# First operands of four stages made in the stages in front, zeros set in parts by VectorE, two norms in one, and VectorE's order in a quantised FFN

## The chip, the cores and the metric

The kernel runs on one core of one Trainium2 chip. The core has a matrix engine (TensorE, PE in the profile), a vector engine (VectorE, DVE), an engine for activation functions (ScalarE, ACT), a general engine (GpSimd, POOL), and a queue engine (SyncE, SP) that issues most transfers between device memory and the on-chip memory SBUF. TensorE writes its results to PSUM. The metric is the time of one execution on the device in microseconds (us), as the median of several runs.

## The reference

The input x is 2048 tokens of 256 numbers, and ctx is a context of the same size. Eight sublayers follow each other, each added to x behind a layer norm without weights:

```
x = x + gamma * cross_attention(norm(x), ctx)             # 8 heads               stage A
x = x + (silu(n @ gate * s) * (n @ up * s)) @ down * s    # 704 wide, ternary     stage B
x = x + quantised_cross_attention(norm(x), ctx)           # 16 heads, 8-bit       stage C
x = x + h + a, a = causal_attention(norm(h)), h = norm(x) # 16 heads of 128       stage D
      + moe(norm(h + a))                                  # 4 experts, top 2
x = x + banded_attention(norm(x), ctx)                    # 8 heads, band of 64   stage E
x = x + bit_linear(silu(w1) * w2, w3)(norm(x))            # 1024 wide, quantised  stage F
x = x + V @ sigmoid(Q^T K)(norm(x), ctx)                  #                       stage G
x = x + moe(norm(x)) + shared(norm(x))                    # 8 experts, top 2      stage H
```

The norm divides by sqrt(variance + 1e-5). Stage D takes two norms in a row: norm(x), and over it a norm with weight and bias. In F each linear layer first takes a root-mean-square norm with a gain, scales the row so that its largest entry becomes 127 (the largest is held at 1e-4 or above), rounds, multiplies by a matrix of -1, 0 and 1, and scales back.

## The kernel before, in words

Tokens lie in 16 tiles `xs[i]` of 128 tokens by 256 numbers that stay in SBUF through the whole kernel, and so do 16 tiles `cs[i]` of the context. Feed-forward stages work on four groups of four tiles (`NG`), with tokens as the matmul's free axis, so they need transposed normed tokens `xnT`. The stages run in the order of `STAGES`; F and G are fused in `run_F`, and `run_G` then returns at once.

The main loop (from L1673) opens the pool of the next stage's weights at the start of the present stage, and its loads are queued on SP there. Pools of successive stages lie on alternate sides of SBUF (`side_of`, L68), counted over all eight letters. As G has a letter of its own, F and H lie on one side, and H's weights are loaded when F is over.

Every engine executes its instructions in the order in which the program issues them. Most stages are therefore written as Python generators that issue a few instructions a step, and a loop over slots steps them beside each other. Where the code says `manual_schedule`, the written order stands; buffers named alike in a pool share memory and wait for each other.

- A (`run_A`, L403): the slots come from `attention_slots` (L330). `start(t)` is called once per slot.
- B (`run_B`, L466): per group, `norm_T` (L505) makes statistics, the normed tiles and their transposes; then six chunks `ic` of the hidden layer with products gp and up, and the down products op (L495). Beside it run keys and values of C (`keys_and_values`, L542), one step at the start and one behind each chunk: product kvp (L568), quantised keys, transposes kTp, kT; at the end the values are scaled by their largest entry (vall, L617) and spread over the zeroed tile vz (L621). vz is zeroed at once by GpSimd (L554).
- C (`run_C`, L644): `queries(i)` (L675) makes the quantised queries of tile i in ten steps; the loop over 256 pairs of tile and head has scores (L759), a row maximum and exponentials on VectorE (L789), ScalarE (L813) and GpSimd (L823), a transposing transfer, and products with vz (L772). `output(i)` (L722) ends a tile.
- D (`load_D` L840, `run_D` L854, `run_D_attention` L920): `inputs(g)` (L934) makes the two norms of one group, one after the other, and the transposes hnT; `values` (L964), `projections` (L974). `run_D_moe` (L1072) has the experts: `hidden(n)` (L1084) and `output(n)` (L1096) for group and expert n, `routed_D` for the next group's routing; beside them run two generators: `tern`, which makes F's ternary matrices (`ternary`, L1260, with a transfer fw, a sum of absolute values L1271, tanh and rounding), and `first`, which makes E's first operands (`first_of_E`, L1169). The latter zeroes and fills eight halves of stk and stq by GpSimd (`operand_buffers`, L148, its line L153).
- E (`run_E`, L1209) uses the same attention slots as A.
- F and G (`run_F`, L1301): software pipeline; a list `parts` (L1505) gives the order of the parts in a period and each one's lag in tiles. `deviations` takes the variance, `scales` (L1335) the scale factors, `first_sizes` (L1345) xk and its largest entries, `gained` (L1404) multiplies the hidden row by its gain on GpSimd (xr, L1409), `second_norm` (L1411) and `second_rounding` (L1417) treat the hidden row.
- H (`load_H` L1557, `run_H` L1578): `owner`, a constant of experts by columns, is built by a memset and six selects on GpSimd (L1586 to L1590); `routed(g)` (L1597) makes a group's norm, transposes, gates and shares; then 14 chunks with pgate and pup (L1649), a broadcast cb of the shares (L1653), and `down` (L1626).

The order of the experts of D around `output`:

```
                next(first if n > 6 else tern, None)
                if e in (1, 2, 3):
                    next(routing, None)
                output(n)
                next(routing, None)
                next(tern, None)
                next(first, None)
```

Of the kernel before, what the change touches and what calls it, by code (L numbers as in the profile page):

```python
# [31 lines left out]
def tile_net(ctx: ExitStack, tc: tile.TileContext, a: dict, out: bass.AP):  # L32
# [31 lines left out]

    beside = []
    pending = []

    def side_of(stage):  # L68
        return ("left", "right")[STAGES.index(stage) % 2]


# [76 lines left out]
    def operand_buffers(pool, k, b, eng=None):  # L148

        pair = {}  # L150
        for kind, value in (("k", 1.0), ("q", 0.0)):
            pair[kind] = pool.tile([P, 16, D], BF, name=f"st{kind}{b}")
            (eng or V).memset(pair[kind][64:P], value)  # L153
        k.setdefault("st", []).append(pair)
# [248 lines left out]
    def run_A(w, side):  # L403
        with ExitStack() as es:
# [6 lines left out]
            masks = []  # L411

            def prepare(i):
# [9 lines left out]
                if i < 4:  # L423
                    operand_buffers(cp, k, i)
# [5 lines left out]
            def start(t):  # L430
                if t in (16, 18):
                    next(parts)
                if t == 20:
                    for r in range(2):
                        masks.append(cp.tile([P, 1], F32, name=f"gmask{r}"))
                        V.tensor_tensor(masks[r], k["mask"][r], w["gamma"], ALU.mult)

# [16 lines left out]
    def load_B(wp):  # L454
# [8 lines left out]
        w["down_s"] = bcast_row(wp, a["L0_ffn_down_s"], D, "sdown")  # L463
        return w

    def run_B(w, side):  # L466
        with tc.tile_pool(name="Bw", bufs=2, side=side) as pool, tc.tile_pool(
            name="Bp", bufs=1, space=PSUM
        ) as psum:
            other, stats = beside.pop() if beside else (iter(()), iter(()))  # L470
            next(other, None)
            for g in range(NG):
                ids = range(4 * g, 4 * g + 4)
                xnT = norm_T(pool, psum, ids)
                hT = pool.tile([P, 6, 512], F32, name="hT")
                for ic in range(6):
# [13 lines left out]
                    next(other, None)  # L490
                for j, i in enumerate(ids):
# [8 lines left out]
                    G.tensor_tensor(xs[i], xs[i], t, ALU.add)  # L500
                next(stats, None)
            for _ in other:
                pass

    def norm_T(pool, psum, ids, src=None, wb=None, keep=None):  # L505
# [3 lines left out]
        xnT = pool.tile([P, 2, 512], F32, name="xnT")  # L509
        for j, i in enumerate(ids):  # L510
# [5 lines left out]
            dst = xnT[:, :, j * P : (j + 1) * P]  # L516
            if wb is None:
                S.copy(dst, tp)
            else:
                for c in range(2):  # L520
                    S.activation(
                        dst[:, c, :], tp[:, c, :], AF.Identity, bias=wb[1][:, c : c + 1], scale=wb[0][:, c : c + 1]
# [4 lines left out]
    def load_C(wp):  # L527
        w = {}
        w["q"] = load(wp, [P, 2, D], a["L1_xattn_Wq"].rearrange("(c p) n -> p c n", p=P), "wq")
        w["kv"] = load(wp, [P, 2, 2 * D], a["L1_xattn_Wkv"].rearrange("(c p) n -> p c n", p=P), "wkv")  # L530
# [7 lines left out]
        w["bkv"] = bcast_row(wp, a["L1_xattn_bkv"], 2 * D, "bkv")  # L538
        w["bp"] = load(wp, [1, D], a["L1_xattn_bp"], "bp")
        w["norm"], w["stats"] = {}, query_stats(w)  # L540
        beside.append((keys_and_values(w), w["stats"]))
        return w  # L542

    def keys_and_values(w):
# [9 lines left out]
        G.memset(vz, 0.0)  # L554
        w["spread"] = spread = qkp.tile([H, 4, 2, 64], F32, name="spread")
        with tc.tile_pool(name="C1v", bufs=1, side=side) as vp, tc.tile_pool(
            name="C1w", bufs=2, side=side
        ) as pool, tc.tile_pool(name="C1p", bufs=1, space=PSUM) as psum:
            vall = vp.tile([P, NT, D], F32, name="vall")
            vm = vp.tile([P, D], F32, name="vmax")  # L560
            V.memset(vm, 0.0)
            for i in range(NT):
# [30 lines left out]
                V.tensor_copy(kT[:, :, i * P : (i + 1) * P], tb)  # L593
                yield
# [1177 lines left out]
```

## Time and profile before

| | us |
|---|---|
| median of 3 runs (2830.92 to 2835.79) | 2834.84 |
| the profiled execution | 2838.68 |
| its span | 2837.0 |
| TensorE busy | 2441.6 (86%) |
| VectorE busy | 1892.7 (67%) |
| ScalarE busy | 1531.6 (54%) |
| GpSimd busy | 1560.0 (55%) |
| A / B / C begin at | 0 / 299 / 531 |
| D's attention / experts begin at | 1229 / 1846 |
| E / F with G / H begin at | 2016 / 2332 / 2522 |

A timeline row has the start in us from the span's start, the duration in us, the engine, the line, the operation, output and input tiles, their shapes, how many like instructions are drawn together (x4), and in brackets how long the engine was idle just before and which instruction ended that. The page also has a table of 40 slices of the span: each digit is the busy share of an engine in tenths, and in the row PEclk the granted clock of TensorE in tenths.

### The profile page before, as it was taken

The page shows a single profiled execution, that of the slowest core. Times are in us where ns is not written, and L with a number is a line of the kernel's source. Part 1 is how long each engine was busy: PE and PEld are TensorE (multiplying, and loading weights), DVE is VectorE, ACT ScalarE, POOL GpSimd, SP SyncE. Part 2 cuts the span into 40 slices and gives each one's busy share as a digit, 9 for nine tenths or more (in the row PEclk, how much of TensorE's full clock was granted, in tenths as well). Part 3 has the DMA queues.
Part 4 walks back from the last instruction along what each step waited for, and adds up shares of the span by engine and source line. Part 5 has one row for each costly group of instructions (what it writes and reads, how often), then busy time and mean ns, then how long its engine had stood idle before and what let it go on. Part 6 is the DMA issues. An engine that isn't in the chain of part 4 may idle for free.

```text
span 2837.0 us, 44436 instructions
## 1 busy us (share of the span) xinstructions
PE 2441.6 (86%) x16072; PEld 1437.3 (51%) x16072; DVE 1892.7 (67%) x3961; ACT 1531.6 (54%) x2186; POOL 1560.0 (55%) x1733
## 2 busy tenths in 40 slices
PE   4989798777787787779999999979898876779999
PEld 2545344344444444336666666746555543445555
DVE  7877555699999999955554555654577759933322
ACT  1667221499999999836555555424255456721111
POOL 4655433488888888856555555442488865630000
PEclk9999799899999999979999999989999999989999
DMA  6553000499999999920000000010343400020000
GB/s 167 134 116 71 23 1 1 85 204 200 205 203 202 200 202 205 206 86 8 16 8 23 8 1 1 15 45 25 83 96 88 95 21 1 1 77 8 8 8 8
DMA packets 610599, 223.70 MB, mean 79 GB/s; under 512 B 547366, under 2 KB 600524, under 8 KB 605772
## 3 DMA queue, kind: packets, MB, share of 16 engines
q1 hardware_dynamic: 607308, 220.07, 35.4%
q8 instruction: 127, 2.08, 0.3%
q10 hardware_dynamic: 3072, 0.79, 0.2%
q14 instruction: 92, 0.75, 0.1%
HBM read 66.91 MB, written 18.87 MB: 30 GB/s over the span
## 4 chain that ended last, share of the span: by engine, by line
PE 48%; DVE 22%; issue 9%; POOL 7%; ACT 2%; DMA 1%; ACTq 0%; DVEq 0%; POOLq 0%; SPq 0%
DVE e L789 11%; PE yp L1042 4%; PE ppq L983 4%; PE ppk L983 4%; PE hout L1628 3%; PE vp L971 3%; PE pgate L1649 3%; PE pup L1649 3%; POOL e L286 2%; PE ep L1104 2%; PE sp L1001 2%; PE op L1027 2%; PE hmp L1091 2%; PE sc L759 1%; PE op L495 1%
## 5 line engine op out<-in xcount | busy, mean ns | idle before, releaser
L813 ACT ACTIVATE ei<-e,nb,sq 128x2048 int16<-128x2048 f32 x256 | 535.4, 2092 | 44.4 <-DVE nb L810 40.8
L823 POOL CAST eb<-ei 128x2048 bf16<-128x2048 int16 x256 | 482.4, 1895 | 117.2 <-ACT ei L813 101.8
L759 PE MATMUL sc<-kT,qz 128*128 128x512 bf16 x1024 | 298.3, 382 | 140.4 <-DVE e L789 138.1
L246 DVE TENSOR_REDUCE negm<-s 128x2 f32<-128x512 f32 (+1 forms) x512 | 300.8, 611 | 127.0 <-PE s L242 123.6
L789 DVE TENSOR_SCALAR_CACHE_REDUCE e<-sc,mx 128x1024 f32<-128x1024 f32 x256 | 326.1, 1274 | 0.8 <-DVE nb L810 0.7
L789 DVE TENSOR_SCALAR_CACHE_REDUCE e<-sc 128x1024 f32<-128x1024 f32 x256 | 312.4, 1220 | 11.5 <-PE sc L759 10.5
L278 ACT ACTIVATE e<-s 128x1024 f32<-128x1024 f32 (+1 forms) x256 | 233.2, 915 | 149.9 <-PE s L274 115.5
L242 PE MATMUL s<-stk,stq 96*128 96x256 bf16 (+1 forms) x1024 | 191.5, 270 | 40.9 <-DMA d3k<-t3k 24.4
L759 PEld LDWEIGHTS <-qz 128*128 128x128 bf16 x1024 | 94.8, 97 | 259.7 <-issue 201.1
L991 POOL TENSOR_TENSOR rwq<-rwq,sin 128x512 f32<-128x512 f32 x64 | 81.2, 1268 | 235.6 <-ACT rwq L988 211.7
L274 PE MATMUL s<-stq,stk 128*128 128x256 bf16 (+1 forms) x1024 | 180.0, 261 | 9.4 <-DMA stq<-nm 4.7
L772 PEld LDWEIGHTS <-vz 128*64 128x64 bf16 x4096 | 123.0, 110 | 115.5 <-issue 115.5
L772 PE MATMUL av<-eT,vz 128*64 128x128 bf16 x4096 | 163.7, 222 | 8.5 <-DMA eT<-eb 8.4
L1003 DVE TENSOR_REDUCE mx<-sp 128x4 f32<-128x512 f32 x64 | 44.3, 692 | 189.9 <-PE sp L1001 189.9
L988 ACT ACTIVATE rwq<-ppq,dbq 64x512 f32<-64x512 f32 x128 | 87.4, 683 | 150.4 <-DVE rtq L985 147.0
L1659 DVE TENSOR_TENSOR hm<-pup,sl 128x512 f32<-128x512 f32 (+1 forms) x56 | 38.7, 692 | 190.4 <-PE pup L1649 186.6
L242 PEld LDWEIGHTS <-stq 96*128 96x128 bf16 x1024 | 93.4, 100 | 135.6 <-issue 111.4
L296 PE MATMUL o<-e,vmo 128*32 128x256 f32 (+1 forms) x2048 | 150.7, 367 | 7.4 <-POOL e L286 6.0
L87 POOL TENSOR_TENSOR rstd<-ve,mhalf 128x1 f32<-128x1 f32 (+1 forms) x52 | 38.1, 733 | 209.3 <-DVE ve L85 90.0
L1657 ACT ACTIVATE sl<-pgate 128x512 f32<-128x512 f32 (+1 forms) x56 | 33.4, 597 | 218.7 <-PE pgate L1649 218.7
L286 POOL TENSOR_SCALAR_AFFINE_SELECT e<-e 128x256 f32<-128x256 f32 (+1 forms) x256 | 133.2, 547 | 30.3 <-ACT e L278 30.1
L971 PE MATMUL vp<-Dwv,hnT 128*128 128x512 f32 x256 | 123.7, 605 | 4.0 <-ACT hnT L946 4.0
(369 smaller groups left out, 5521.8 us busy)
## 6 DMA issues: line engine op xcount, KB each, us to landing
stk<-d3k SPq DMA_DIRECT2D x96, 192.0 KB
stq<-d3q SPq DMA_DIRECT2D x96, 192.0 KB
d3k<-t3k SPq DMA_DIRECT2D x160, 64.0 KB
d3q<-t3q SPq DMA_DIRECT2D x96, 64.0 KB
eT<-eb SPq DMA_TRANSPOSE x256
fw<-in_L_ffn_w SPq DMA_DIRECT2D x3, 1024.0 KB
x<-in_x SPq DMA_DIRECT2D x16, 128.0 KB
c<-in_ctx SPq DMA_DIRECT2D x16, 128.0 KB
```

The lines of the kernel that those rows point to most:

```text
L242: PE.matmul(sc[:, hh, lo:hi], qs[0:96, 2 * hp + hh, qc * P : (qc + 1) * P], ks[0:96, 2 * hp + hh, lo:hi], start=band is None, stop=True, s ...
L246: V.tensor_reduce(negm[:, qc, 2 * hp : 2 * hp + 2], sc[:, :, lo:hi], AX.X, ALU.max, negate=True)
L274: PE.matmul(sc[:, c, lo:hi], ks[:, h, lc * P : (lc + 1) * P], qs[:, h, lo:hi], start=True, stop=True)
L278: S.activation(e[:, :, lo:hi], sc[:, :, lo:hi], AF.Exp, scale=scale)
L286: G.affine_select(e[:, :, s0:s1], e[:, :, s0:s1], [[0, 4], [step, s1 - s0]], ALU.is_ge, 0.0, base=base, channel_multiplier=chan,)
L759: PE.matmul(sc[:, k0 : k0 + 512], qz[i % 2][:, h, :], kT[:, h // 2, 1024 * part + k0 : 1024 * part + k0 + 512], start=True, stop=True,)
L772: PE.matmul(av[i][r0 : r0 + 64, h // 4, :], vz[:, kt, h // 4, h % 4, :], eT[:, kt, :], start=h == 0 and kt < 2, stop=h == H - 1 and kt >= ...
L789: V.tensor_scalar(e, scs.pop((n, part)), 1.0, mx[:, 0:1] if part else LOWEST, ALU.mult, ALU.max, accum_out=mx[:, part : part + 1],)
L813: S.activation(ei, es_.pop(n), AF.Exp, bias=nb, scale=sq[i][:, h : h + 1], accum_out=sums[i][:, h : h + 1],)
L823: G.tensor_copy(eb, eis.pop(n - 1))
L971: PE.matmul(vp, hnT[g][:, c, j * P : (j + 1) * P], wv[:, c, :], start=c == 0, stop=c == 1)
L983: PE.matmul(pp, wt[:, c, hh * P : (hh + 1) * P], hnT[g][:, c, :], start=c == 0, stop=c == 1)
```

## The change

1. **First operands ahead.** A dictionary `heads` holds generators that a stage's loader leaves for the stage in front. B's first group (`norm_parts`) is stepped in A's slots from t = 146; C's first tile (`queries_of_C`, with zeroing of qz and scaling of the weights) at the end of the generator that runs in B; D's first group (`inputs_D`) in C's tail from n = 256 and between the steps of the last `output`; H's first group (`routed_H`) in F's tail from t = 17.
2. **Sides.** They are counted over "ABCDEFH", so F and H lie on opposite sides and H's weights are loaded while F runs. `owner` is made by three copies on ScalarE from the identity matrix. In H, the routing of the next group is issued in steps, one a chunk, from chunk 3.
3. **B.** vz is zeroed a tile at a time, in each step of `keys_and_values`. Its last part is split by more yields, and `run_B` calls it more often at its end (two steps a chunk in the last group, one behind each of the last eight outputs, one more at g = 1). wkv and bkv are loaded by the generator.
4. **D's norms.** `inputs_D` takes one set of statistics per tile: with variance v, the second norm's factor follows from (v + 1e-5) * 1e-5 + v. One pow makes both factors. The expert weights we1, be1, be2 are loaded behind the first group's attention weights instead of in front of them; the first columns of wv are loaded with the stage's small weights.
5. **D's experts.** E's zeros and ones are set by VectorE, one memset per step. `output` is split in two halves, and `another()` steps one generator behind the hidden layer and behind each half. `ternary` issues the next matrix's load earlier, and takes its sum in two halves.
6. **F.** The scale factors are made by a pow and a multiplication on GpSimd (`factors`), with the constants folded in; `scales` has two VectorE instructions less with two operands. The order of `parts` is changed.

The diff, cut to its core:

```diff
+    SEQ = STAGES.replace("FG", "F")
     def side_of(stage):
-        return ("left", "right")[STAGES.index(stage) % 2]
+        return ("left", "right")[SEQ.index(stage) % 2]
+    heads = {}
...
-    def operand_buffers(pool, k, b, eng=None):
+    def operand_buffers(pool, k, b):
...
-            (eng or V).memset(pair[kind][64:P], value)
+            V.memset(pair[kind][64:P], value)
+            yield
...
+                if t == 146 and "B" in heads:
+                    head.append(heads.pop("B")(pool, psum))
+                if head:
+                    next(head[0], None)
...
+        w["xnT0"] = wp.tile([P, 2, 512], F32, name="xnT0")
+        heads["B"] = lambda pool, psum: norm_parts(w["xnT0"], pool, psum, "tp", range(4))
...
+                if g == 1:
+                    next(other, None)
-                xnT = norm_T(pool, psum, ids)
+                xnT = norm_T(pool, psum, ids, dst=None if g % 2 else w["xnT0"], bufs=1) if g else w["xnT0"]
...
-                    next(other, None)
+                    for _ in range(2 if g == 3 else 1):
+                        next(other, None)
...
+                    if g >= 2:
+                        next(other, None)
...
+    def norm_parts(dst, pool, psum, tag, ids):
+        mv, rstd = ln_stats(pool, [xs[i] for i in ids], "hd")
+        yield
+        for j, i in enumerate(ids):
+            xn = pool.tile([P, D], F32, name="hdn", bufs=2)
+            ln_apply(xn, xs[i], mv, rstd, j)
+            yield
+            S.copy(dst[:, :, j * P : (j + 1) * P], transpose_to(psum, xn, tag, f"hdT_{i}"))
+        yield
...
-        G.memset(vz, 0.0)
...
                 V.tensor_copy(kT[:, :, i * P : (i + 1) * P], tb)
+                G.memset(vz[:, i], 0.0)
                 yield
...
+        for b in range(2):
+            V.memset(w["qz"][b], 0.0)
+        S.mul(w["q"], w["q"], 0.25)
+        S.mul(w["bq"], w["bq"], 0.25)
...
+            yield from queries_of_C(w, 0, pool, qzp, psum)
...
-                for _ in queries(0):
-                    pass
...
+                    if n == N and "D" in heads:
+                        own = dict(stats=(small, H, "amq"), bn=(small, H, "rsq"), h0=(pool, D, "xn"), h1=(pool, D, "qq"))
...
+                        head = heads.pop("D")(tile, psum)
+                    if n >= N:
+                        next(head, None)
                 for _ in out_:
+                    next(head, None)
+                for _ in head:
                     pass
...
+    def inputs_D(w, hs, hnT, g, tile, psum):
...
+            V.bn_stats(b6, xs[4 * g + j])
+            V.bn_aggr(mv[:, j, :], b6)
...
+        V.tensor_scalar(ve[:, 0, :], mv[:, :, 1], 1e-5, None, ALU.add)
+        V.scalar_tensor_tensor(ve[:, 1, :], ve[:, 0, :], 1e-5, mv[:, :, 1], ALU.mult, ALU.add)
+        G.tensor_tensor(r, t[:, 8:16], mhalf[:, 0:8], ALU.pow)
...
             ahead = routed_D(w, hs, 0, pool, psum, "vy")
             weights_of(0)
-            inputs(0)
+            if "D" in heads:
+                heads.pop("D")
+                inputs(0)
+            else:
+                mv, rstd = ln_stats(pool, [xs[j] for j in range(4)])
+                for j in range(4):
+                    ln_apply(hs[j], xs[j], mv, rstd, j)
+                    G.tensor_tensor(hs[j], hs[j], w["bo"], ALU.add)
+            w["experts"]()
...
+            def another():
+                q = next(slots)
+                next(tern if q % 8 >= 4 and q < 24 or q == 24 else first, None)
...
-                next(first if n > 6 else tern, None)
+                another()
...
-                output(n)
+                output(n, 0)
+                another()
+                output(n, 1)
                 next(routing, None)
-                next(tern, None)
-                next(first, None)
+                another()
...
+            def factors(t, n, nm):
+                r = pool.tile([P, 1], F32, name=f"r{nm}")
+                G.tensor_tensor(r, t[:, n : n + 1], mhalf[:, 0:1], ALU.pow)
+                f = pool.tile([P, n + 1], F32, name=f"f{nm}")
+                G.tensor_scalar(f, t, r, 1.0, ALU.mult, ALU.mult)
+                return f
+            def scales(am, f, n, nm):
-                V.tensor_scalar(am, am, s, 1e-4, ALU.mult, ALU.max)
+                V.tensor_scalar(am, am, 1.0 / 127.0, f[:, n : n + 1], ALU.mult, ALU.max)
                 sc = pool.tile([P, n], F32, name=f"sc{nm}")
                 V.reciprocal(sc, am)
-                V.scalar_tensor_tensor(sc, sc, 127.0, s.to_broadcast([P, n]), ALU.mult, ALU.mult)
                 dq = pool.tile([P, n], F32, name=f"dq{nm}", bufs=4)
-                V.tensor_tensor(dq, am, at_, ALU.mult)
+                V.tensor_tensor(dq, am, f[:, 0:n], ALU.mult)
...
             parts = [
                 (summed, 5), (first_transposes, 1), (first_copy, 1), (second_transposes, 4), (second_copy, 4),
-                (hidden, 2), (g_product, 7), (g_sum, 7), (hidden_products, 1), (gates, 1), (second_norm, 3),
-                (squares, 2), (gained, 2), (g_context, 6), (g_context_copy, 6), (first_sizes, 0), (first_rounding, 0),
-                (second_rounding, 3), (g_scores, 6), (g_tanh, 6), (output, 4), (deviations, -1), (g_norm, 5),
+                (second_factors, 3), (first_sizes, 0), (hidden, 2), (g_product, 7), (g_sum, 7), (hidden_products, 1),
+                (gates, 1), (squares, 2), (gained, 2), (g_context, 6), (g_context_copy, 6), (first_rounding, 0),
+                (second_sizes, 3), (deviations, -1), (g_deviations, 5), (second_rounding, 3), (first_factors, -1),
+                (g_norm, 5), (g_scores, 6), (g_tanh, 6), (output, 4),
             ]
...
+                    if with_g and t >= NT + 1 and part.__name__ == "gained":
+                        next(heads.get("owner", head), None)
+                    if with_g and t >= NT + 1 and "H" in heads:
+                        head = heads.pop("H")(pool, psum, ("l0", "l1"), "sl")
+                    if t >= NT + 1 and part.__name__ in ("g_sum", "g_tanh"):
+                        next(head, None)
...
+    def owners(owner):
+        for t in range(3):
+            rows = slice(32 * t, 32 * t + 32)
+            S.copy(
+                owner[rows].rearrange("p (e i) -> p e i", i=176), bc(ident[rows, 32 * t : 32 * t + 8], 2, [32, 8, 176])
+            )
+            yield
...
-                    if ch == 5 and g + 1 < NG:
-                        nxt = routed(g + 1)
+                    if ch == 3 and g + 1 < NG:
+                        nxt = routed_H(w, g + 1, pool, psum, ("tp", "tp"), "xn4")
+                    next(nxt, None)
```

## The prediction

> **What bounds the kernel now.** I read the page's table of slices first, for where TensorE goes slack, then the timeline around each of those places.
>
> ```profile
> PE   4989798777787787779999999979898876779999
> ...
> PEclk9999799899999999979999999989999999989999
> ```
>
> One slice is 70.9 us. TensorE is nearly full over long stretches; it is lower between stages, in F (slices 32 to 35) and in C (7 to 17), where VectorE sets the pace at 2.56 us a head and nothing is changed. The change works on the seams and on F, so the sum goes seam by seam.
>
> ```profile
> 298.60 13.75 POOL L554 MEMSET vz<- 128x16384 bf16 x1
> 301.04 11.34 DVE L85 TENSOR_SCALAR ve<-mv 128x4 f32<-128x4 f32 x1
> 330.80 2.07 PE L482 MATMUL gp<-xnT,wgate 128*128 128x512 f32 x4
> ...
> 520.88 0.72 POOL L500 TENSOR_TENSOR x<-x,t 128x256 f32<-128x256 f32 x1 [2.84 <-DVE t L499]
> 530.89 1.23 DVE L789 TENSOR_SCALAR_CACHE_REDUCE e<-sc 128x1024 f32<-128x1024 f32 x1 [5.65 <-PE sc L759]
> ...
> 1217.86 0.72 POOL L752 TENSOR_TENSOR x<-x,ops 128x256 f32<-128x256 f32 x1
> 1229.11 1.92 PE L971 MATMUL vp<-Dwv,hnT 128*128 128x512 f32 x2
> ...
> 1862.17 7.28 DVE L91 TENSOR_SCALAR hn<-h,mv,rstd 128x256 f32<-128x256 f32 x2 [0.74 <-POOL rstd L87]
> 1865.64 3.65 POOL L153 MEMSET stq<- 64x4096 bf16 x1
> 1869.88 3.78 PE L1104 MATMUL ep<-we,hm 128*128 128x256 f32 x8 [6.38 <-DVE h L1107]
> ...
> 2401.34 0.42 DVE L1326 BATCH_NORM_STATS2 b<-x 128x6 f32<-128x256 f32 x1
> 2406.79 2.49 POOL L1409 TENSOR_TENSOR xr<-h,fg 128x512 f32<-128x512 f32 x2
> 2407.01 1.06 DVE L1340 SCALAR_TENSOR_TENSOR sca<-sca,s 128x2 f32<-128x2 f32 x1
> 2410.69 0.42 DVE L1326 BATCH_NORM_STATS2 b<-x 128x6 f32<-128x256 f32 x1
> ...
> 2503.12 0.72 POOL L1503 TENSOR_TENSOR x<-x,gy 128x256 f32<-128x256 f32 x1 [3.01 <-ACT gy L1502]
> 2521.92 3.76 PE L1649 MATMUL pgate<-xnT,hwgate 128*128 128x512 f32 x4
> ```
>
> The blocks are the seams A to B, B to C and C to D, D's experts, F's loop, and the seam to H. Each seam shows the last operation of the old stage or the load in the way, then the first of the new. The bracket is idle time of that engine and what ended it. Two things stand out: a tiny VectorE instruction takes 11.34 us beside the 13.75 us GpSimd memset (the same 128x4 operation takes 0.15 at 313.69), and 7.28 us cover two multiplies that take 0.73 elsewhere (1226.53) beside GpSimd memsets of 3.5. So each large GpSimd memset holds VectorE for its length.
>
> **The change, part by part**, against the profiled execution of 2838.68 us (span 2837.0), which is 3.84 us above the median 2834.84.
>
> **A to B, 26 us.** The first group's norm, transposes and zeros leave the head of B. A's last chain ends with VectorE's reciprocal of the denominators at 295.06, so with xnT0 made in A's tail the first gp can start at about 296 instead of 330.80: 34.8 us. TensorE was not empty in that gap: keys and values of context tiles took about 8 us there (three products kvp of 1.9 each, transposes), which now stand in B's loop. That loop was 102.0 of 110 us busy from 350 to 460, so I hide none of it: 34.8 - 8 = 26.8, less about 1 for the norm's small instructions in A's tail. The memset becomes 16 parts of about 13.75/16 = 0.86, each holding VectorE that long at most, under a loop in which VectorE had 61.2 and GpSimd 40.2 of 110 busy; queued behind each piece on GpSimd is the next tile's kk, which came 0.5 to 3 us after idle time there, so I cost the pieces at nothing, and at 16 x 0.86 = 14 if that cover fails. The load of wkv, now issued by the generator itself, is still ahead of its first use on SP's queue (the first kvp waited 4.33 us for it at 299.85, inside the gap); it stays hidden if issued while A runs. Bounds: 15, if the pieces wait in A's tail or VectorE's holds reach TensorE, and 31, if half of the 8 goes into gaps and TensorE stays warm (it had a granted clock of 0.58 from 294.7 to 330.8).
>
> **B to C, 8.3 us.** The last x of B starts at 520.88, the first e at 530.89. Zeros, scaling and queries of tile 0 now run in B's tail, so what is left is the last product, the release of its PSUM and one score chunk (529.82 to 530.89, 1.07): about 522.5. Against it, ten query steps are added to B's tail, where the splitting of the values left TensorE 5.65 us idle in 460 to 482 (16.35 of 22). I count the two as level. Bounds 5 to 9.
>
> **C to D, 6 us.** Last x to first vp: 11.25 us. Both norms in one take out one round of statistics, a pow (1.0) and a multiply; for group 0 the chain leaves D's head. But its steps share with C's last output the one small PSUM buffer, so C's tail becomes longer: I put the first vp at about 1223. Bounds 1 (the chain only moves ahead of the last output) and 11 (all of it hidden). The moved loads: the expert weights no longer stand in SP's queue in front of the attention's; Dwv's first columns are there early, Dwq is then the one that may be late.
>
> **D's experts, 15 us.** E's eight memsets go from GpSimd to VectorE: four of 3.47 and four of 1.77 (rows of the same tiles in A), 20.9 us of VectorE time, one per slot. VectorE then has some 40 us of work in the first expert group against 33.5 for TensorE. Without GpSimd's locks (7.28, 4.59 and others), with output split in two and the ternary weight fetched ahead (a reduce waited 7.70 us for its DMA at 1898.26), I walk the first group to 54 us instead of the 69.5 from its first product to the next group's. Groups behind took 34 to 41 and stay. Bounds 5 (VectorE's memsets cost as much as the locks did) and 25 (down to the later groups' length).
>
> **E's start, 4 us.** Its first statistics at 2021.05 wait 3.81 us and a score 5.27; with E's first operands done earlier, this goes. Bounds 0 to 6.
>
> **F, 12 us.** A period is 9.35 us (2401.34 to 2410.69) and VectorE is 94% busy in it. The row sca shows the loss: 1.06 us beside GpSimd's xr, where scb, blocked by nothing, takes 0.16. In the new order no two-operand VectorE instruction lies under xr, and two scale multiplies move to GpSimd (0.21 to 0.28 each there). VectorE's period in the new order: 9.35, less 0.90 for the blocked sca, less 0.32 for two multiplies of 0.16 that leave it, plus 0.29 for longer forms of those that stay (an estimate), 8.42, so 0.93 a period; the loop over TensorE and ScalarE needs 8.0 to 8.4 and limits any more. 15 periods are 14; I take 12, as the first and last are not bound by VectorE. Bounds 0 and 17.
>
> The Trainium skill has the rule behind this ("SBUF — State Buffer", section "Who interferes with whom"): VectorE's second port pair is GpSimd's, a VectorE instruction with two SBUF inputs is shut out by a GpSimd one that reads SBUF, and "not with one that only writes it". sca agrees. The rule also speaks against the change: the new factors are GpSimd reads and stand in front of xk, which has two SBUF inputs. That result is rival 1.
>
> **F to H, 15 us.** TensorE's last product in F ends at 2502.4 and pgate starts at 2521.92: 19.5. H's weights (5.44 MB, 2503.9 to 2522) now load during F, when DMA stood at 0.00 of its share, and routing for group 0 runs in F's tail; the owner tile's selects on GpSimd (11 us) become three copies on ScalarE. About 1.5 more as the cold first pgate (3.76, later 1.88) is warm. Against it F's tail gets the routing's pieces, a table load of 1.28 (perhaps two) and copies of some 1.4 on the engine that closes the loop (an estimate between 0.60 for 512 elements, L1657, and 2.09 for 2048, L813): 6. Bounds 9 and 22.
>
> **Sum**: 26 + 8.3 + 6 + 15 + 4 + 12 + 15 = 86.3. 2838.7 - 86.3 = 2752 on the profiled scale, 2749 with the 3.84 us to the median; I say 2750.
>
> **Rivals.**
> 1. The ports shut each other out in F in another place: GpSimd's factors beside VectorE's xk. For it: 0.5 us of GpSimd multiplies a period are new there. Against it: at 2358.50 a pair of xk kept its usual 0.87 beside a GpSimd pow of 0.72 (0.55 elsewhere), so little is lost. F then gains nothing: 2762.
> 2. The heads are made early but the next stage still waits, for memory or PSUM of the old pools or for the weights that are loaded behind it. For it: at 1218.61 the statistics waited for the very last x though group 0 was long done. Half of the four seams' 55 us is lost, and some of D's: 2750 + 28 + 10 = 2788. This is also the case that the change does not do what it says.
> 3. TensorE stays warm and the neighbours gain as well: clock rows of 0.58 (A to B), 0.68 (2016 to 2032) and 0.56 (2503 to 2522) go to 1. With the upper bounds for A to B, experts and the last seam (5 + 10 + 7) and some for C to D: 2722.
> 4. Slower: B's loop turns serial. A tile's keys are a chain of 12.6 us (transposes at 401.16, end of the kT copy at 413.76) over all four engines, beside 6.9 us from one step of the loop to the next. Two tiles overlap now; with GpSimd's memset at the end of each step and steps in other places, a tile could wait for the one before. If each of 16 stood in full, 16 x (12.6 - 6.9) = 91 > 86, so 2750 + 91 = 2841. It decides from about 15 of 16 standing. Before, the same steps ran at 93% TensorE occupancy, which speaks against it.
>
> By the Trainium skill ("TensorE: Matmul & The Clock Gate", Part 1) the clock halves after about 3.4 us of idleness and returns after as much work; pgate's 3.76 against 1.88 agrees. By that rule every seam that closes below 3.4 us would also give back the cold products behind it.
>
> **How the numbers follow.** Forecast (2735 to 2772, with rival 1 in it) 0.65, of which rival 1 has 0.15; rival 2 0.15; rival 3 0.15; rival 4 0.05. The range, from rival 3's value to a little past rival 2's, 2720 to 2794, leaves the slower case and the outer halves of both wings out. A measurement of this kernel tells 0.2% (5.7 us) from no change: faster than that 0.93, within 0.02, slower 0.05.
>
> **What would show it.** Right: gp starts at about 296, the first e within 2 us of B's last product, vp by 1224, no VectorE row of several us for a small norm in D's experts, F's period at 8.4, pgate within 2 us of the last gop, H's weights moving during F. Wrong: any seam still open by over 8 us; a period of 9 or more with long xk rows; an idle column of several us in B's loop; GpSimd memsets of vz holding VectorE in rows where TensorE waits.

## The result, and the profile after

The changed kernel took 2784.93 us (median of 4 runs, 2780.02 to 2786.97) against 2834.94 for the kernel before (4 runs): a ratio of 0.9824, 95% interval 0.9807 to 0.9841. That is 50 us less; the forecast was 85 less. The profiled execution took 2783.10 (span 2781.4), 1.83 below its median, where that of before lay 3.84 above its own; so the two traces stand 55.6 us apart, and the stretches below are of the traces.

The two rows of slices of the changed kernel's page (one slice is now 69.5 us):

```profile
PE   4999899778778778779999999979898887789999
...
PEclk9999999999999999989999999989999998989999
```

TensorE's dips at A to B (slice 5, from 7 to 8) and around the end of F (slices 33 to 36) are smaller, not gone. The kernel cut at the same operations in both traces, each stretch from one start to the next (us):

| stretch | before | after | predicted gain | gain |
|---|---|---|---|---|
| start to B's first gp | 330.8 | 293.4 | | 37.4 |
| B, first gp to last down sum | 189.6 | 209.3 | 26 with the row above | -19.7 |
| to C's first e | 10.5 | 1.6 | 8.3 | 8.9 |
| C, first e to last e | 665.4 | 664.4 | 0 | 1.0 |
| C's end, last e to last x | 21.6 | 27.4 | | -5.8 |
| to D's first vp | 11.2 | 0.0 | 6 with the row above | 11.2 |
| D's attention, to first hmp | 617.3 | 620.2 | 0 | -2.9 |
| D's experts, to last ep | 166.4 | 156.8 | 15 | 9.6 |
| E, with the seams beside it | 320.0 | 316.8 | 4 | 3.2 |
| F's loop, first to last b | 124.7 | 113.0 | 12 | 11.7 |
| F's end, last b to last gop | 44.6 | 62.6 | | -18.0 |
| to H's first pgate | 19.9 | 1.3 | 15 with the row above | 18.6 |
| H, to its last product | 310.8 | 310.3 | 0 | 0.5 |

The first gp starts beside the reciprocals of A's last chain (293.33) instead of 36 us behind them. These come between 290.5 and 296.3 in the kernels below, though A's own work is the same in all of them, so of the 37.4 of the first row 35.7 are the seam's and 1.7 are such spread. But GpSimd's zeros, now in pieces, stand almost all together at the head of B. The timeline of the changed kernel at A to B:

```profile
293.35 1.98 PE L501 MATMUL gp<-xnT,wgate 128*128 128x512 f32 x4 [0.51 <-ACT rd L314]
...
304.93 4.52 POOL L628 MEMSET vz<- 128x1024 bf16 x5
305.02 4.89 DVE L95 TENSOR_SCALAR xn<-x,mv,rstd 128x256 f32<-128x256 f32 x2 [1.21 <-POOL rstd L91]
...
311.27 0.66 PE L101 MATMUL cT<-ident,c 128*128 128x128 f32 x2 [5.35 <-DVE vall L605]
```

All 16 pieces start between 293.4 and 314.0, although the program issues one per context tile. So "in the order in which the program issues them", as it was said of the engines, is too strict for this kernel: outside the stretches with a manual schedule, the order in a queue is not the written one, and these traces show instructions that wait for nothing standing further ahead than they were written. Five of the pieces hold VectorE's norm of the second group for 4.89 us, and TensorE idles for 5.35 us behind it. The seams to C and to D:

```profile
502.67 0.42 DVE L519 TENSOR_TENSOR t<-op,sdown 128x256 f32<-128x256 f32 x1 [1.66 <-PE op L515]
504.27 1.21 DVE L840 TENSOR_SCALAR_CACHE_REDUCE e<-sc 128x1024 f32<-128x1024 f32 x1
...
1196.08 4.13 PE L1066 MATMUL vp<-Dwv,hnT 128*128 128x512 f32 x9 [0.52 <-ACT ops L803]
1196.10 0.72 POOL L805 TENSOR_TENSOR x<-x,ops 128x256 f32<-128x256 f32 x1 [7.22 <-ACT ops L803]
```

Both are closed: the first e comes 1.6 us after the last sum of B, and vp starts with the last x of C. D's experts have no GpSimd memset any more, but VectorE's stand where the locked rows stood:

```profile
1833.19 3.47 DVE L157 MEMSET stk<- 64x4096 bf16 x1 [0.91 <-issue]
1837.04 1.76 DVE L157 MEMSET stq<- 64x2048 uint32 x1 [0.37 <-issue]
1838.84 0.73 DVE L95 TENSOR_SCALAR in_h<-h,mv,rstd 128x256 f32<-128x256 f32 x2
1839.49 0.87 DVE L1210 SCALAR_TENSOR_TENSOR h<-ep,comb,h 128x256 f32<-128x256 f32 x2
1840.02 3.78 PE L1207 MATMUL ep<-we,hm 128*128 128x256 f32 x8 [6.87 <-DVE h L1210]
```

The norm in_h is down from 7.28 to 0.73, yet TensorE waits 6.87 us for the sum h, which frees its PSUM; it waited 6.38 there before. F's period and the end of F:

```profile
2394.25 2.50 POOL L1551 TENSOR_TENSOR xr<-h,fg 128x512 f32<-128x512 f32 x2
2394.35 0.42 DVE L1460 BATCH_NORM_STATS2 b<-x 128x6 f32<-128x256 f32 x1
...
2395.92 0.85 DVE L1484 TENSOR_TENSOR dqb<-amb,fb 128x1 f32<-128x1 f32 x1
...
2398.18 0.87 DVE L1491 SCALAR_TENSOR_TENSOR xk<-x,mv,fg 128x256 f32<-128x256 f32 x2
2398.42 0.70 POOL L1475 TENSOR_SCALAR fa<-basea,ra 128x3 f32<-128x3 f32 x1
...
2402.93 0.42 DVE L1460 BATCH_NORM_STATS2 b<-x 128x6 f32<-128x256 f32 x1
```

```profile
2459.58 1.02 PE L1790 MATMUL combT<-ident,comb 128*8 128x128 f32 x4 [2.68 <-DVE comb L1786]
2460.39 0.63 PE L1615 MATMUL gcT<-ident,c 128*128 128x128 f32 x2
...
2463.71 2.46 PE L1650 MATMUL gop<-gsg,cT 128*64 128x256 f32 x8 [0.67 <-ACT gsg L1641]
```

The period is 8.2 and 8.6 in turn, 8.4 on average as worked out. One row was not in that working: dqb, a VectorE instruction with two operands, now stands under xr and ends with it. It takes 0.48 to 1.04 us in the last six periods of the loop; in the kernel before it stood behind xr:

```profile
2409.90 0.15 DVE L1342 TENSOR_TENSOR dqb<-amb,watanh 128x1 f32<-128x1 f32 x1
```

In the second fence of the two above, the last tile's transpose gcT, which belongs to F, stands in TensorE's queue behind combT, which belongs to H and waits for VectorE's choice of the two experts. The last gop comes 18 us later relative to the last b than before, about what the seam behind it gained.

### The profile page after: what moved, and what is told of

Same layout as the page of the kernel before. It is cut to its first block, busy times and chain, and to the rows that moved or that the text cites. A ratio compares the mean times of both kernels' runs of the same rounds, so it can differ in the third digit from the quotient of the medians.

```text
span 2781.4 us, 44370 instructions
## 1 busy us (share of the span) xinstructions
PE 2432.0 (87%) x16078; PEld 1432.5 (52%) x16078; DVE 1876.9 (67%) x3919; ACT 1531.5 (55%) x2181; POOL 1533.9 (55%) x1764
## 4 chain that ended last, share of the span: by engine, by line
PE 47%; DVE 20%; issue 9%; POOL 5%; ACT 2%; DMA 1%; ACTq 0%; SPq 0%; POOLq 0%; DVEq 0%
DVE e L840 11%; PE yp L1137 4%; PE ppq L1078 4%; PE ppk L1078 4%; PE pgate L1836 4%; PE pup L1836 3%; PE hout L1812 3%; PE vp L1066 3%; PE sp L1096 2%; PE op L1122 2%; POOL e L291 2%; PE ep L1207 2%; PE hmp L1194 2%; PE sc L812 1%; PE op L801 1%
## 5 line engine op out<-in xcount | busy, mean ns | idle before, releaser
L91 POOL TENSOR_TENSOR rstd<-ve,mhalf 128x1 f32<-128x1 f32 (+1 forms) x40 | 25.8, 646 | 182.8 <-DVE mv L424 69.2
```

## The experiments

Each kernel is the changed kernel with one edit, unless it says otherwise; each was timed in five rounds beside the kernel before. Differences to the changed kernel are between medians of two sets of runs; every ratio is to the kernel before. As the changed kernel's own runs lie up to 7 us apart, a difference of a few us is read from the stretches of the traces and not from the median. Stretches are named and cut as in the table above.

The theory after the first reading: what the moved heads gain is given back because the moved work stands in queues in front of the old stage's own work. The rivals: F's new order made F's end longer; and B is longer only because of the keys and values that moved into it.

**h_off.** The hook in F's list of parts is removed; routing and owner copies run at H's head.

```diff
-                    if with_g and t >= NT + 1 and part.__name__ == "gained":
-                        next(heads.get("owner", head), None)
-                    if with_g and t >= NT + 1 and "H" in heads:
-                        head = heads.pop("H")(pool, psum, ("l0", "l1"), "sl")
-                    if t >= NT + 1 and part.__name__ in ("g_sum", "g_tanh"):
-                        next(head, None)
```

> The changed kernel, with the routing of H's first group and the three copies of owner taken out of F's tail: both stand at the head of H again, while H's weights still load during F. Theory 1: the pieces in F's tail made it longer (last statistics b to last gop 62.6 us, 44.6 before), as they stand in queues in front of F's own work. Without them that stretch is about 48, and the seam from the last gop to the first pgate, now 1.3, becomes about 12: together some 4 us less, 2781 against 2785. Rival: F's new order made the tail longer; then the stretch stays near 60, the seam becomes 12, and the kernel is about 10 us slower, 2795.

Measured: 2773.33 us, ratio 0.9789 (0.9776 to 0.9803): 11.6 us faster than with the head. F's end is 46.1, and the seam 2.9, not 12; F's loop is 3.9 longer (116.9), so the three together are 11.0 shorter. The theory held and was too modest, since the seam hardly reopened. The timeline of this kernel shows why:

```profile
2376.64 0.41 DVE L95 TENSOR_SCALAR xn<-x,mvh,rstdh 128x256 f32<-128x256 f32 x1 [1.02 <-POOL rstdh L91]
...
2454.85 1.57 PE L1650 MATMUL gop<-gsg,cT 128*64 128x256 f32 x8 [0.67 <-ACT gsg L1641]
2457.06 0.66 PE L1766 MATMUL hnT<-ident,xn 128*128 128x128 f32 x4 [0.65 <-ACT gy L1657]
2458.44 0.66 PE L1766 MATMUL hnT<-ident,xn 128*128 128x128 f32 x4 [0.72 <-ACT xnT L1767]
2458.93 1.02 PE L1829 MATMUL pgate<-xnT,hwgate 128*128 128x512 f32 x2
2459.79 1.93 PE L1772 MATMUL hgp<-hgate,xnT 128*128 128x8 f32 x16
```

H's norm of the first group (mvh, xn) is in F's loop at 2376.64, and the second group's at 2412.99, without a line that puts them there: with H's memory on the other side they wait for nothing of F but x, and stand further ahead than they were written. Softmax and shares then run beside the first gate products. In the changed kernel the hook holds the same norm back:

```profile
2434.44 0.72 DVE L95 TENSOR_SCALAR sl<-x,mvh,rstdh 128x256 f32<-128x256 f32 x2
```

The group's last sum x was made at 2368.22 there. So the head that was stepped by hand made the first group's norm later, not earlier, and put it into F's end.

**h_split.** `routed_H` is cut behind the transposes; the second half is a generator of its own that runs at H's head.

```diff
-        heads["H"] = lambda ...: routed_H(w, 0, pool, psum, tags, big)
+        heads["H"] = lambda ...: normed_H(w, 0, pool, psum, tags, big)
...
+            for _ in shares_H(w, 0, pool, psum, ("tp", "tp")):
+                pass
```

> The changed kernel, with H's first routing cut in two: norm and transposes stay in F's tail, the gate products, the softmax, the choice of two and the shares are issued at H's start, where gate and up products can run beside them. Theory 1: what costs most in the tail is the chain of softmax and shares (TensorE waits 2.7 us for comb, a table load of 1.3, VectorE's small steps in front of F's): last b to last gop falls from 62.6 to about 54, the seam grows from 1.3 to about 5, some 5 us less, 2780. Rival: the tail's length comes from F's order or from the norm and the owner copies: no difference, 2785, or a few us more where the gate products now delay H.

Measured: 2778.01, ratio 0.9808 (0.9795 to 0.9821), 6.9 faster; F's end 54.4 and the seam 2.8. So the chain of softmax and shares is about half of the 16.5 us between 62.6 and 46.1; norm, transposes and owner copies are the rest, of which 3.9 go into F's loop when the hook is gone (113.0 here, 116.9 in h_off).

**f_old.** F's scale factors and list of parts as before; all else is the changed kernel.

> The changed kernel, with F's order of parts and its scale factors as they were before; H's first routing is still stepped in F's tail and its weights load during F. Theory 1: the new order gave 11.7 us from the first to the last statistics b and did not touch the tail: about 12 us more, 2797. Rival: the new order also made the tail longer, by about what it saved in the loop: no difference, 2785, with the stretch from last b to last gop near 52 instead of 62.6.

Measured: 2796.71, ratio 0.9870 (0.9854 to 0.9885), 11.8 slower. The rival falls as to the time: F's new order and factors are worth their 12 us. But half of its stretch is there: F's end is 56.9 with the old order, so the new one made it 5.7 longer. The loop alone gains 19 (132.3 against 113.0) with H's statistics beside it; see the run after next.

**vz_dve.**

```diff
-                G.memset(vz[:, i], 0.0)
+                V.memset(vz[:, i], 0.0)
```

> The changed kernel, with the 16 zeroings of vz issued to VectorE instead of GpSimd. Theory 1: all sixteen stand together at the head of B in GpSimd's queue (13.7 us from 293 to 315) and hold VectorE's norm for 4.89 us and TensorE for 5.35; on VectorE they take about 0.45 us each and lie apart: about 6 us less, 2779, the stretch from first gp to last down sum 203 instead of 209. Rival: the longer B comes from the keys and values that moved into it and TensorE would have waited anyway: within 2 us of 2785.

Measured: 2769.53, ratio 0.9782 (0.9766 to 0.9798), 15.4 faster. B is 199.0, so the zeros on GpSimd cost it 10.3; what is left, 199.0 - 189.6 = 9.4, is near the 8 that the prediction gave to the moved keys and values. The tile's groups:

```profile
L628 DVE MEMSET vz<- x16: 485/485/485, 292.9 to 352.1; 128x512 uint32 x16
```

Half as long a piece as GpSimd's 0.955, and spread over 59 us. The other 5 us of the median are not B's: 2.5 of them are in H, which took 307.8 here and 310.3 in the changed kernel with the same code. H's first 52 us had a granted clock of 0.95 in the latter and 1.00 in the former. The other runs with this H fall on the same two sides: 307.8 at 1.00 in e_pool, d_off and b_off, 310.1 and 310.7 at 0.96 and 0.94 in c_off and f_old.

**sides.** The kernel before, with `side_of` and the main loop counted over "ABCDEFH", and nothing else.

> The kernel before, with one edit alone: the sides are counted over ABCDEFH, so that H's weights load during F and H's memory is not F's. Nothing is stepped ahead by hand. Theory 1: this alone closes most of the seam, as H's first norm, constants and transposes are no longer held by F's memory or by the load: from 19.9 us between the last gop and the first pgate to about 4, some 16 us less than before, 2818 against 2834. Rival: the pieces of H that flow forward into F cost there what they save, as in the changed kernel: 2832 to 2836.

Measured: 2838.80 (12 runs), ratio 1.0022 (1.0013 to 1.0030): slower. The rival held, in more than its size. The seam falls to 7.0, but F's loop grows from 124.7 to 141.3 and its end to 49.4. Its timeline in F:

```profile
2405.42 0.93 POOL L1505 TENSOR_TENSOR x<-x,gy 128x256 f32<-128x256 f32 x1 [0.98 <-ACT gy L1504]
2406.39 0.43 DVE L84 BATCH_NORM_STATS2 bnst<-x 128x6 f32<-128x256 f32 x1 [0.62 <-POOL x L1505]
2406.73 0.67 DVE L1353 TENSOR_REDUCE am<-xk 128x2 f32<-128x512 f32 x1
2406.83 2.49 POOL L1411 TENSOR_TENSOR xr<-h,fg 128x512 f32<-128x512 f32 x2
2407.32 0.17 DVE L85 BATCH_NORM_AGGREGATE mv<-bnst 128x2 f32<-128x6 f32 x1
2407.43 0.69 DVE L1339 TENSOR_SCALAR am<-am,s 128x2 f32<-128x2 f32 x1
```

The statistics bnst of H (0.43 and 0.17) have moved into the engine that bounds F, wait there for the period's x, and push F's small scalings under xr (am 0.69; 0.23 before, at 2406.55). The period goes from 9.35 to 10.6 or 11.2, once to 12.9. So the same move that feeds H for nothing in h_off costs here more than it saves; in the new order of F there is room for it (116.9 in h_off).

**best1.** vz_dve and h_off together.

> The changed kernel with both edits that gained: zeros of vz by VectorE, and H's first routing not stepped in F's tail. If the two are independent, as stages A to C and F to H are, their gains add: 2785 - 15.4 - 11.6 = 2758. Rival: part of the gain of either was the chance of one run's timing: 2765 or more.

Measured: 2763.22, ratio 0.9752 (0.9740 to 0.9765), between the two. B is 198.3 and F's end 46.3, so both edits keep their stage's gain. Most of the 5 us short of the sum is the spread of the medians: the profiled executions give 14.1 and 7.5 for the two edits apart and 19.9 together, 1.7 short. H takes 310.8 here, as in h_off, at a granted clock of 1.00 in its first 52 us; in both it has the first group's softmax and shares beside it.

**e_pool.**

```diff
-            yield from operand_buffers(cp, w["k"], b)
+            yield from operand_buffers(cp, w["k"], b, G)
```

> The changed kernel with E's eight memsets back on GpSimd, still one per step. Theory 1: GpSimd's memsets hold VectorE's norms again, rows of 3 to 7 us come back, and the experts (first hmp to last ep) grow from 156.8 us to about 163, as the other edits there keep their part: some 6 us more, 2791. Rival: the gain of the experts comes from the split outputs and the early load of the ternary weight, and VectorE's memsets cost what the locks did: within 2 us of 2785.

Measured: 2772.76, ratio 0.9783 (0.9771 to 0.9796): 12.2 faster, where both theories had slower or the same. Experts 146.7, E with its seams 2.0 longer (318.8). Both theories fall. Its timeline:

```profile
1830.58 7.28 DVE L95 TENSOR_SCALAR in_h<-h,mv,rstd 128x256 f32<-128x256 f32 x2 [1.21 <-POOL rstd L91]
1830.60 3.51 POOL L157 MEMSET stk<- 64x4096 bf16 x1
1834.05 3.65 POOL L157 MEMSET stq<- 64x4096 bf16 x1
...
1858.27 3.51 POOL L157 MEMSET stk<- 64x4096 bf16 x1
1858.36 0.48 DVE L1210 SCALAR_TENSOR_TENSOR h<-ep,comb,h 128x256 f32<-128x256 f32 x1 [0.38 <-PE ep L1207]
```

The lock is there, once, at in_h. But the sum h, which TensorE waits for, takes its usual 0.48 beside a memset. No VectorE row beside the other six memsets is longer than elsewhere, and TensorE waits for h only once for longer than 1.4 us, 6.62 at 1838.29. With the memsets on VectorE it waits three times behind them, for 6.87, 5.10 and 1.69 us.

**d_off.** `if n == N and "D" in heads:` becomes a condition that never holds.

> The changed kernel with D's first group not stepped in C's tail: its norm, in the one-pass form, and its transposes stand at D's head. Theory 1: C's end (last e to last x) shrinks from 27.4 us to about 22, its length before, and the seam from last x to first vp grows from 0 to about 9, since the one-pass norm leaves 2 of the 11.2 away: some 4 us more, 2789. Rival: the norm flows forward into C's tail by the order of issue as H's did, so the hand-written head gains nothing: 2783 to 2786.

Measured: 2780.20, ratio 0.9812 (0.9798 to 0.9826), 4.7 faster by the median, where theory 1 had it slower and the rival the same. C's end is 21.7, as theory 1 had it, the seam 6.6 and not 9: the head that is stepped by hand saves 6.6 us in the seam and costs 5.7 in C's end, so it gains 0.9, and of the 5.4 that C to D gained 4.5 come from the single norm. The 4.7 us of the median are elsewhere (B 1.6 shorter, H 2.5), so no cost of the head is shown.

**best2.** vz_dve, h_off and e_pool together.

> The changed kernel with three edits: zeros of vz by VectorE, H's first routing not stepped in F's tail, and E's memsets on GpSimd, one per step. Theory 1: the three lie in different stages and add: 2763 for the first two, less the 10 us that the experts (first hmp to last ep) were shorter with the third (146.7 against 156.8): 2753. Rival: the shorter experts only uncover the next wait, E's first operands, as E began no earlier against its last score: 2758 or more, with E or the seam to it longer.

Measured: 2753.69, ratio 0.9717 (0.9703 to 0.9730): 31 us faster than the changed kernel, as the sum had it. E took 304.4 from its first score to its last product (303.8 in the changed kernel), so nothing was uncovered.

**b_off.** The condition `t == 146` in A never holds.

> The changed kernel with B's first group not stepped in A's tail: its norm and transposes stand at B's head, beside GpSimd's zeros of vz. Theory 1: the head is worth most of what this seam gained. The first gp comes at about 318 instead of 293, as the norm is held by the zeros; keys and values run in that gap, so B from first gp on is 11 us shorter (198); some 14 us more, 2799. Rival: the norm flows forward into A by the order of issue, as H's did into F, and the zeros in parts are what removed the gap: first gp by 300, 2785 to 2788.

Measured: 2789.54, ratio 0.9843 (0.9829 to 0.9856), 4.6 slower. The first gp is at 316.4 and B takes 197.7, as theory 1 had both, though its 2799 was 9 too high; the two together are 11.4 worse than the changed kernel, 1.0 of it because A's last chain came later, and differences of 2.5 in H and 1.2 in F's loop make the median less. The head is worth some 10.4 in its place. In this kernel's trace it is again GpSimd's zeros that hold the norm:

```profile
304.16 2.74 POOL L628 MEMSET vz<- 128x1024 bf16 x3
304.25 3.11 DVE L95 TENSOR_SCALAR hdn<-x,mvhd,rstdhd 128x256 f32<-128x256 f32 x2 [0.90 <-POOL rstdhd L91]
```

**c_off.** `queries_of_C(w, 0, ...)` leaves the generator of keys and values; C's head calls it.

> The changed kernel with C's first queries made at C's head again; qz is still zeroed and the weights scaled in B's tail. Theory 1: the seam from B's last down sum to the first e grows from 1.6 us back to about 10, and B (first gp to last down sum, 209.3) shrinks by at most 3, as the ten query steps lie in gaps of TensorE: some 6 us more, 2791. Rival: the queries are part of what made B longer, B shrinks by 8 or more and nothing is gained by moving them: 2783 to 2787.

Measured: 2790.81, ratio 0.9848 (0.9835 to 0.9862), 5.9 slower; seam 10.6, B 210.2. B is no shorter without the first queries, so they cost it nothing.

**best3.** best2, with E's second pair of memsets and two steps of the ternary weights exchanged.

```diff
-                next(tern if q % 8 >= 4 and q < 24 or q == 24 else first, None)
+                next(tern if q % 8 in (2, 3, 4, 5) and q < 24 or q == 24 else first, None)
```

> The kernel with the three edits (zeros of vz by VectorE, H's first routing at H, E's memsets on GpSimd), and with another order of the two generators beside the experts: E's second pair of memsets, which held VectorE's in_h for 7.28 us and TensorE for 6.6 in the run with the memsets on GpSimd, changes places with two steps of the ternary weights. Theory 1: a GpSimd memset holds only VectorE's in_h and small scalings, not the sums h (0.48 us beside one), so with no memset beside in_h that row is 0.73 and the experts are 6 us shorter (140 against 146.6): 2748 against 2754. Rival: the two sums of absolute values (1.2 us each) that now stand there hold the sums h instead, or another memset meets in_h later: 145 or more, 2752 or more.

Measured: 2752.86, ratio 0.9724 (0.9709 to 0.9739), the same as best2; experts 146.7. The rival held, by its second half:

```profile
1820.92 0.73 DVE L95 TENSOR_SCALAR in_h<-h,mv,rstd 128x256 f32<-128x256 f32 x2
...
1855.19 7.28 DVE L95 TENSOR_SCALAR in_h<-h,mv,rstd 128x256 f32<-128x256 f32 x2 [1.13 <-POOL rstd L91]
1855.22 3.51 POOL L157 MEMSET stk<- 64x4096 bf16 x1
1858.66 3.65 POOL L157 MEMSET stq<- 64x4096 bf16 x1
```

The lock left the first group's in_h and caught the second's, with the same 7.28. That the length of in_h is set by the memsets beside it is shown by this; that it can be avoided altogether was not.

## Why the prediction was right or wrong

The sign was right, and the time lies inside the range; the forecast of 2750 was 35 us too low, and 2784.93 lies outside the 2735 to 2772 that had most of the chance. The range held because it reached past rival 2, and as rival 2 is not what happened, that is luck in part. On the traces the gain is 55.6 where 86.3 was put, and 28 of the 31 missing are in three steps: A to B, D's experts, and F to H. With those three mended (best2) the time is 2753.69. By its steps:

1. **A to B** (26; 17.7, or 16.0 without the spread of A's end). The first gp came where it was put. The step that failed is "I cost the pieces at nothing": the pieces were taken to lie one per tile, but in GpSimd's queue they stand together at the head of B. The fallback price that the step named, 14, was nearer: vz_dve shows 10.3. The sign of being wrong that the prediction named for it, memsets of vz that hold VectorE where TensorE waits, is there (4.89 and 5.35). The remaining 9.4 fit the 8 us of moved keys and values, but no run took these apart.
2. **B to C** (8.3; 8.9) and **C to D** (6; 5.4): right, in the terms as well (C's end 5.8 longer). But most of the gain at D is that of the single norm; moving it ahead gave about 1.
3. **D's experts** (15; 9.6). The step that failed is the walk that weighed VectorE's 20.9 us of memsets against the locks as times of a busy engine. What counts is what stands in front of h. With the memsets on GpSimd the other edits gave 19.7, and the move to VectorE cost 10.1 of it. The walk put the first group at 54 us: it took 62.7 with VectorE's memsets and 52.5 with GpSimd's, so the memsets are the term that was wrong. The lower bound named for it, "VectorE's memsets cost as much as the locks did", was too kind to VectorE: its memsets cost 10.1 more than the one lock of e_pool, and 9.6 was left only because the other edits gave more than was put.
4. **F** (12; 11.7): right in the sum, and f_old gives the same by another way; not in every term. "In the new order no two-operand VectorE instruction lies under xr" is not so: dqb does, and takes back 0.3 to 0.9 of the 0.90 a period that sca gave free, and H's statistics (bnst and mvh) stand in the last three periods of the loop. That the period is 8.4 all the same is luck in part: savings that the sum did not list make up for them. Rival 1, xk shut out by the new factors, did not occur, but its mirror image did: xk keeps 0.87, and GpSimd's fa beside it takes 0.70 instead of 0.27. That fits the Trainium skill ("SBUF — State Buffer", section "Who interferes with whom"), by which it is the order of issue that decides who blocks.
5. **F to H** (15; 0.6). The seam closed by 18.6 of its 19.9, but F's end grew by 18.0 where 6 was put. The step that failed is "F's tail gets the routing's pieces": they were priced by their own durations, and not by what waits behind them. A piece that waits for another engine makes the work of F that is queued behind it wait as well, as gcT behind combT. h_off shows 16.5 of the 18.0 to come from the moved pieces; without them 3.9 go into F's loop and 1.6 into the seam, and 11.0 are won.
6. **E** (4; 3.2): about right. **D's attention** lost 2.9, which was not predicted. It stands in every kernel with the new C to D, also without the head (621.5 in d_off). The loss lies in the first 64 us, where TensorE waits 5.56 for a row s of VectorE's softmax (3.00 before) and 4.90 for hnT (3.26 before); which edit makes these waits longer was not tried.

Rival 2 (heads made early, and half the gain lost) is the nearest to what happened in size, but not by its mechanism: the first product of no new stage waited for more than 0.65 us (gp 0.51, vp 0.52, pgate 0.65). Rival 3 did not come, and rival 4 is excluded by B's 209.3.

## What to carry to other kernels

Work that is moved ahead of a seam must be priced by what stands behind it in each queue of the old stage, not by its own length: here a head that closed a seam of 19.9 us lengthened the stage in front by 18. Of the four heads, B's gave some 10.4 us in its stretches and C's 9.0 in its seam, D's 0.9, and H's cost 11.0. Where an engine is waited for, look at which of its instructions the others need: a slow memset on another engine that blocks only a norm was cheaper by 10 us in D's experts than a fast one in the queue of the sums. And before stepping work ahead by hand, see whether it moves by itself once its memory is free, and into which engine's time: in h_off it did, some 58 us earlier than by hand.

## What the runs showed of the hardware

Beside two GpSimd memsets of 3.51 and 3.65 us, two of VectorE's norms (a tile in SBUF by two factors per row) took 7.28 us together (0.73 alone), and the sum h, with one operand in PSUM, its usual 0.48 beside another of 3.51. Beside GpSimd's xr (two rows, 2.50 us), VectorE's dqb on 128 by 1 numbers took up to 1.04 us (0.15 alone) and ended when xr did. VectorE's memset to zero went as uint32 and took 1.77 us for a tile of 64 by 4096 bf16, to one as bf16 3.47; GpSimd took 3.5 to 3.65 for either. H took 307.8 us, or 310.1 to 310.7, in runs with the same code, with a granted clock of 1.00, or 0.94 to 0.96, in its first 52 us; what decides between the two was not tried.
